# A four-layer graph network on one core: records placed by one-hot matmuls, neighbour products ahead of self products, early gathers among the scatters

## The chip, the core and the metric

The kernel runs on one core of one Trainium2 chip. The metric is the device time of one execution in microseconds (us), smaller is better. PE is the matrix engine, PEld its weight loads, DVE is VectorE, ACT is ScalarE, POOL is GpSimd, SP is the engine that issues plain DMAs. Line numbers L… are those of the kernel before.

## The reference

A graph of 3,327 nodes has 512 features per node (`x`) and a 0/1 matrix `adj` with about four ones in each row. Four layers follow one another, each as `x = x + layer(relu(layernorm(x)), adj)`:

```
layer 0:  deg = sum(adj, 1);  agg = adj @ h / max(deg, 1)
          out = relu(concat(h @ W_self + b_self, agg @ W_nb + b_nb) @ W_comb + b_comb)
layer 1:  8 heads of 64:   Wh = h @ W;  e = leaky_relu(Wh·a_src + (Wh·a_dst)^T), masked by adj
          out = softmax(e) @ Wh
layer 2:  the same with 4 heads of 128 and W made of four signed blocks; out = elu(...)
layer 3:  the same with one head of 512
```

A node without a neighbour attends in layers 1 to 3 to all nodes alike. Everything is float32.

## The kernel before, in words

The kernel never multiplies by `adj`. It finds the neighbours of each node, sorts the nodes by their number of neighbours (most first), and then gathers neighbours' rows from a table in device memory. The 3,328 rows (one is padding) are 26 chunks of 128. After sorting, `slots_of` says how many neighbour slots a chunk needs at most: 14 for chunk 0, 8 for chunk 1, 7 for 2 and 3, 6 for 4 to 6, 5 for 7 to 10, 4 for 11 to 15, 3 for 16 to 20, 2 for 21 to 23, 1 for 24 and 25; together 117. If the data does not fit these limits, a flag sends the kernel to a general path, which does not run here.

**Stage 0** (up to 264 us) works on the nodes in their given order. `SEQUENCE` (L606) is the order of the chunks. For each chunk,

- `look` (L1189) loads the rows of `adj`, and VectorE finds the columns with a one (`max_index`, L1209: four finds a chunk, 104 in all);
- `lists` (L1226), for groups of chunks, makes the node numbers from the finds and counts the degrees on VectorE; POOL writes each node's record: 16 neighbour numbers, its own number and its degree (`records`, L1259);
- `x` is loaded, normalised (statistics L1309, the refinement of 1/sigma L831 to L836), put through relu, transposed by PE (L1337), copied to `hT` (L1342) and multiplied by the two folded weights (L1349): the neighbour product goes through `zt` to `table[0]` (L1366), the self product into the node's row in SBUF (L1373). Each product is four matmuls of K = 128, which the trace shows as eight rows.

A node's row in SBUF (`node(i)`, 1,042 words) is x, self product and record. Ten chunks lie in `early`, sixteen in `later`; `later` also holds the weights while they are being folded, so these rows wait for room (`free_at`).

When all finds are done, VectorE counts the nodes of each degree with two small matmuls (L1406, L1410), and a scan and a reduction give every node's place (`places`, L1415; the result `ranki` ends the step). Then POOL scatters the 26 chunks' rows to `own` in device memory (`scatter`, L1434, one indirect DMA of 128 rows each), SP reads the records back in sorted order (`back`, L1450), and VectorE makes 1/degree from them (L1505, L1506). The places are also written beside the rows of `table[0]` (L1467), so that a gathered row brings its node's sorted place with it.

**Layer 0** (to 448 us) goes over the sorted chunks in units of one or two (`ORDERS[0]`). For each slot of a chunk POOL gathers 128 rows from `table[0]` into one of the 33 slots of `ring` (`gather`, L1545; line L1562 issues). VectorE notes the neighbours' places for the other layers (`nbr`, L1862). PE sums a part of the slots in PSUM by multiplying with the identity (`sum_on_pe`, L1584; L1593); VectorE then scales by 1/degree and adds the self product from the own row (L1871), adds the bias (L1879), adds the rest of the slots one by one (L1887; `ON_DVE` gives up to five of them to VectorE), and makes the new x (L1895). The own row (x and self product, `xy`) is loaded by SP from `own` (L1854). `project` (L1602) makes the next layer's table: statistics (L1649), normalisation, four transposes (L1694), copies (L1705), 16 rows of matmul (L1780), copies, and a store (L1822).

**Layers 1 to 3** (`attend`, L1911) gather from `table[layer]` by `nbr` after all rows of that table are stored (POOL's `mark`, L2194, waits for them). VectorE computes the softmax over the slots (L1941 to L1978), VectorE (L2110) and ACT (L2096) multiply the slots with the weights (`ON_ACT` says how many slots ACT takes), PE (and in layer 1 VectorE) sums them. In layer 3 VectorE sums, PE multiplies, and POOL scatters the result to the output (L2072).

**The order of the work** is written out at build time by `Plan` (L614): every step has an engine, a cost, a rank, what it waits for and which buffers it takes and gives; `run` repeatedly takes the step that can start first by these costs (ties by rank) and emits it. Each engine then runs its steps in that order. There is one plan for stage 0 and one for the four layers. Scatters are put behind the first plan as a list:

```
for i in SEQUENCE:
    scatter(i)
back()
degrees()
```

Of the kernel before, what the change touches and what calls it, by code (L numbers as in the profile page):

```python
# [8 lines left out]
F32 = mybir.dt.float32  # L9
# [9 lines left out]
P = 128  # L19
# [7 lines left out]
def general_path(  # L27
# [519 lines left out]
    def l3_finish(pc, i, o):  # L547
# [19 lines left out]
RING = 33  # L567
NEVER = -1.0e30
# [11 lines left out]
        (24,), (12, 21), (11,), (6,), (18,), (17,), (15,), (4,), (3,), (20,), (5, 9), (22,), (10, 19), (1,),  # L580
        (2,), (14,), (0,), (23,), (8,), (13, 16), (7,), (25,),
    ),
    1: (
        (18, 21), (22, 24), (15,), (5,), (10, 20), (2,), (17,), (12, 23), (19,), (4,), (9, 14), (7,), (11, 16),
        (8, 13), (6,), (1,), (0,), (3,), (25,),
    ),
    2: (
        (18, 23), (19, 24), (16,), (20,), (6, 11), (10, 14), (7, 12), (5, 13), (9,), (1,), (21, 22), (4,), (0,),
        (8,), (2,), (3,), (15,), (17,), (25,),
    ),  # L590
    3: (
        (0,), (7,), (17,), (15, 20), (25,), (11,), (3,), (23,), (1, 5), (24,), (4, 14), (16,), (12, 22), (8,),
        (9,), (10,), (18,), (2,), (13,), (19,), (21,), (6,),
# [5 lines left out]
    2: {S: S // 5 for S in range(1, SLOTS + 1)},  # L599
}  # L600

SUMMED = {1: False, 2: False, 3: False}
EARLY = 10
# [6 lines left out]
ORDER_W = {1: -20.0, 0: -1.0, "bias": -4.0, "later": 20.0}  # L610
ADJ, WORK, WORK0, X0, X, SELF = 1.0, 1.13, 1.2, -14.0, 1.77, 7.0


class Plan:  # L614
# [5 lines left out]
    def __init__(self, limits):  # L620
        self.ops = []
        self.limits = limits
        self.taker = {}
# [26 lines left out]
    def run(self):  # L650
        free = {}
# [41 lines left out]
def gnn_stack_kernel(  # L693
# [30 lines left out]
    ROW = 2 * D + SLOTS + 2  # L724
# [10 lines left out]
    with ExitStack() as st:  # L735
# [8 lines left out]
        own = dram.tile([NP, ROW], F32, tag="own", name="own")  # L744
# [30 lines left out]
        nc.gpsimd.iota(node_i, pattern=[[P, NK]], base=0, channel_multiplier=1)  # L775
        eps = const.tile([P, 1], F32, tag="eps", name="eps")
# [19 lines left out]
        srec_f = big.tile([P, NK, SLOTS + 2], F32, tag="srec", name="srec")  # L796
        srec = srec_f.bitcast(I32)
# [17 lines left out]

        biasf = big.tile([P, D], F32, tag="biasf", name="biasf")
# [35 lines left out]
        with tc.tile_pool(name="p0", bufs=1) as pa, tc.tile_pool(name="p0p", bufs=2, space=PSUM) as pp:  # L852
# [4 lines left out]
            early = pa.tile([P, EARLY, ROW], F32, tag="early", name="early")  # L857
            later = pa.tile([P, NK - EARLY, ROW], F32, tag="later", name="later")

            def node(i):  # L860
                return early[:, i, :] if i < EARLY else later[:, i - EARLY, :]

            spare = later.rearrange("p k w -> p (k w)")
# [5 lines left out]
            def part(name, *shape):  # L869
# [6 lines left out]
                assert spare_at[0] <= (NK - EARLY) * ROW  # L876
# [22 lines left out]
            def free_at(i):  # L899

                lo = (i - EARLY) * ROW
                return [o for (a, b), o in users if i >= EARLY and a < lo + ROW and b > lo]
# [7 lines left out]
            limits = {"ai": AI, "h": 2, "hT": 3, "pt": 2, "pz": 2, "py": 2, "pm": 2, "zt": 2, "mv": 3, "norm": 3, "st": 2, "fo": 2}  # L910
# [315 lines left out]
            def lists(rank, i0, i1, found):  # L1226
# [32 lines left out]
                def records():  # L1259
                    none = pa.tile([P, GROUP, SLOTS], F32, tag="none", name=f"none{i0}", bufs=2)[:, :n, :]  # L1260
                    nc.gpsimd.tensor_scalar(none, nid[:, i0:i1, :], 0.0, null_f[:, 1:2], ALU.is_equal, ALU.mult)
                    nc.gpsimd.tensor_tensor(none, none, nid[:, i0:i1, :], ALU.add)
                    for j in range(n):
                        rec = node(i0 + j)[:, 2 * D :].bitcast(I32)
# [4 lines left out]
                        )  # L1269

                room = [o for i in range(i0, i1) for o in free_at(i)]
                return listed, put("pool", 0.6 + 0.75 * n, rank, records, (), [listed] + room)

            recorded = {}
            listed = []
# [984 lines left out]
```

## Time and profile before

| what | us |
|---|---|
| median of 11 runs (lowest, highest) | 1072.61 (1071.53, 1078.27) |
| the profiled execution, its span | 1079.16, 1077.1 |
| PE, DVE, ACT, POOL busy | 877.9, 724.8, 518.1, 621.0 |
| last find ends; places ready | 208.4; 220.5 |
| first, last scatter | 221.6, 258.1 |
| records back, first gather | 268.6, 269.4 |
| marks: tables of layers 1, 2, 3 whole | 448.2, 653.3, 869.3 |
| last transfer to the output issued | 1065.1 |

Matmuls are pipelined and their ends are modelled: an engine's busy share is an average over stages with different limits, and a busy PE is not PE at its peak. DMA share is the mean over 16 engines.

### The profile page before, as it was taken

Reading aid. Unit: us, or ns where it says so; the run is one execution under the profiler, and the core shown is the slowest. Engines: PE = TensorE matmul, PEld = TensorE weight load, DVE = VectorE, ACT = ScalarE, POOL = GpSimd, SP = SyncE. Lnnn points to the kernel's source line nnn. Section 1 sums busy time; section 2 is a strip of 40 time slices with the busy share of each in tenths; the row PEclk is TensorE's granted clock in tenths of the full one; section 3 lists DMA queues with packets and bytes.
Section 4 is the critical chain, followed back from the end, with each engine's and each line's share of the span. In section 5 each row is a group of like instructions: output and inputs, shape, how many; then the busy total and the mean of one; then the engine's idle time right before and its main releaser. Section 6 shows DMA issues by size and latency. Waiting matters only on the chain. (4 is left out here: it accounts for less than half of the span.)

```text
span 1077.1 us, 11605 instructions
## 1 busy us (share of the span) xinstructions
PE 877.9 (82%) x2853; PEld 499.1 (46%) x2853; DVE 724.8 (67%) x1848; ACT 518.1 (48%) x1700; POOL 621.0 (58%) x719
## 2 busy tenths in 40 slices
PE   7599999995799998658999983897989815949885
PEld 4244444442376665536666652443544412414332
DVE  6399988830697769278999882787885708435541
ACT  3398877631353533436677641654664602213221
POOL 1051444673777773177787704788787057677771
PEclk9799999998899999869999996897988856979888
DMA  9999888399999986278777604767766146677671
GB/s 348 318 357 384 310 291 316 104 296 327 298 339 301 355 274 218 75 198 234 227 214 214 184 30 131 202 192 203 221 178 185 43 123 195 188 205 207 192 200 54
DMA packets 89911, 240.51 MB, mean 223 GB/s; under 512 B 24933, under 2 KB 26477, under 8 KB 89834
## 3 DMA queue, kind: packets, MB, share of 16 engines
q0 software_dynamic: 41600, 137.72, 43.3%
q1 hardware_dynamic: 48234, 101.96, 26.8%
q8 instruction: 25, 0.41, 0.2%
q14 instruction: 52, 0.43, 0.1%
HBM read 190.35 MB, written 49.27 MB: 222 GB/s over the span
## 5 line engine op out<-in xcount | busy, mean ns | idle before, releaser
L1562 POOL DMA_INDIRECT ring<-table,nbr x351 | 379.0, 1080 | 115.7 <-issue 60.4
L1593 PE MATMUL acc<-ring,ident 128*128 128x512 f32 (+1 forms) x494 | 257.3, 656 | 75.8 <-DVE ring L2110 48.5
L1780 PE MATMUL pw<-w,hT 128*128 128x264 f32 (+1 forms) x832 | 194.0, 390 | 2.1 <-ACT hT L1705 2.1
L1780 PEld LDWEIGHTS pw<-w,hT 128*128 128x128 f32 x832 | 159.8, 193 | 41.8 <-ACT hT L1705 8.5
L1593 PEld LDWEIGHTS acc<-ring,ident 128*128 128x128 f32 (+1 forms) x494 | 95.3, 208 | 180.0 <-issue 81.3
L1562 POOL DMA_INDIRECT ring<-table,srec x117 | 110.3, 943 | 45.7 <-issue 20.7
L2110 DVE TENSOR_TENSOR ring<-ring,w 128x2048 f32<-128x2048 f32 (+7 forms) x76 | 114.4, 1532 | 1.8
L1941 DVE TENSOR_TENSOR e<-ring,fs 128x24 f32<-128x24 f32 (+25 forms) x96 | 15.1, 171 | 133.6 <-DMA ring<-table,nbr 126.3
L2060 PE MATMUL pw<-w,hT 128*128 128x512 f32 x208 | 101.4, 634 | 4.2 <-ACT hT L2052 4.2
L1209 DVE FIND_INDEX8 fidx<-one_i,ai 128x8 uint32<-128x832 int32 x104 | 104.2, 1018 | 0.0
L1217 ACT ACTIVATE junk<-ai 128x1664 int8<-128x1664 int32 (+1 forms) x52 | 82.7, 1591 | 34.1 <-DMA ai<-in_adj_dram 33.8
L1349 PE MATMUL pz_n<-wf,hT_n 128*128 128x512 f32 x208 | 92.3, 595 | 2.9 <-ACT hT_n L1342 2.9
L1349 PE MATMUL py_n<-wf,hT_n 128*128 128x512 f32 x208 | 91.9, 592 | 0.0
L1705 ACT ACTIVATE hT<-pt 128x128 f32<-128x128 f32 (+1 forms) x312 | 81.9, 292 | 19.2 <-PE pt L1694 18.6
L2060 PEld LDWEIGHTS pw<-w,hT 128*128 128x128 f32 x208 | 41.8, 204 | 62.0 <-issue 48.5
L1705 ACT ACTIVATION_READ_ACCUMULATOR hT<-pt 128x1 f32 x312 | 69.4, 223 | 0.0
L822 ACT ACTIVATE ln<-mv,eps 128x1 f32<-128x1 f32 (+1 forms) x60 | 18.0, 300 | 98.5 <-DVE mv L1650 90.3
L1349 PEld LDWEIGHTS pz_n<-wf,hT_n 128*128 128x128 f32 x208 | 39.0, 190 | 52.5 <-issue 45.7
L2046 PE MATMUL pt<-ident,y 128*128 128x128 f32 x96 | 15.4, 293 | 57.6 <-DVE y L2030 52.1
L1968 ACT ACTIVATE ex<-el 128x48 f32<-128x48 f32 (+19 forms) x56 | 12.8, 232 | 101.1 <-DVE el L1951 101.1
L2194 POOL MEMSET mark<- 1x1 f32 x3 | 0.3, 88 | 106.0 <-DMA table<-t 106.0
L2030 DVE SCALAR_TENSOR_TENSOR acc<-ring,w,acc 128x512 f32<-128x512 f32 (+2 forms) x67 | 50.5, 753 | 13.6 <-ACT acc L2028 12.0
(185 smaller groups left out, 1321.0 us busy)
## 6 DMA issues: line engine op xcount, KB each, us to landing
ai<-in_adj_dram SPq DMA_DIRECT2D x25, 832.0 KB, 7.5
ai<-in_adj_dram SPq DMA_DIRECT2D x25, 831.5 KB, 7.6
table<-t SPq DMA_DIRECT2D x52, 258.0 KB, 3.6
xy<-own SPq DMA_DIRECT2D x26, 512.0 KB, 6.0
table<-t SPq DMA_DIRECT2D x26, 260.0 KB, 4.9
table<-zt_n SPq DMA_DIRECT2D x26, 256.0 KB, 5.8
ring<-table,nbr POOLq DMA_INDIRECT x351, 3.7
later<-in_x_dram SPq DMA_DIRECT2D x15, 256.0 KB, 6.8
```

The costliest lines, as they stand in the source:

```text
L822: nc.scalar.activation(ln, var, AF.Ln, bias=eps, scale=scale)
L1209: nc.vector.max_index(fidx[:, i, qq * 8 : (qq + 1) * 8], one_i, ai[:, q * QW : min(cols, (q + 1) * QW)])
L1217: nc.scalar.activation(junk[:, :cols], tiles["ai", key][:, :cols], AF.Square, accum_out=sq[:, i, hf : hf + 1])
L1349: nc.tensor.matmul(pz, tiles["hT", key][:, c, :], wf[s][:, c, :], start=(c == 0), stop=(c == DC - 1))
L1562: nc.gpsimd.indirect_dma_start(out=ring[:m, r0 + s, : width[layer]], out_offset=None, in_=table[layer], in_offset=bass.IndirectOffsetOnAxi ...
L1593: nc.tensor.matmul(acc, ident[:m, :], g[:m, s, :D], start=(k == 0), stop=(k == len(slots) - 1))
L1705: nc.scalar.activation(hT[:, c, :n], pt[:, c, :n], AF.Copy, accum_out=hsum[layer][:, i, c : c + 1])
L1780: nc.tensor.matmul(pw[:, b, :w], tiles["hT", key][:, c, :], wsb[layer][:, c, b, :w], start=(c == 0), stop=(c == DC - 1),)
L2030: nc.vector.scalar_tensor_tensor(to[:m, :], row, weight, acc[:m, :], ALU.mult, ALU.add)
L2046: nc.tensor.transpose(pt[:, c, :], tiles["y", key][:, c * P : (c + 1) * P], ident)
L2060: nc.tensor.matmul(pw[:, 0, :], tiles["hT", key][:, c, :], w3[:, c, :], start=False, stop=(c == DC - 1))
L2110: nc.vector.tensor_tensor(v, v, box["w"][:m, j, lo:hi, :].unsqueeze(3).to_broadcast([m, hi - lo, H, O]), ALU.mult,)
```

## The change

1. **Sort on chip.** The records are no longer part of a node's row. POOL writes them to `record` in SBUF as two parts: seven words (five neighbours, node number, degree) and nine more neighbours, which only the first seven sorted chunks can have. When the places are known, VectorE splits each into chunk and lane, masks the records by chunk into 245 columns, and makes a one-hot matrix of the lanes; 26 matmuls add the records up in their sorted places in PSUM; four copies bring them to `srec` and 1/degree to `rdeg`. The read `back` and `degrees` go.
2. **Rows of 1,024 words.** `own` holds x and self product alone. The ring is allocated from the start and takes the place of `later`: chunks from the eleventh of `SEQUENCE` on and the weights lie in it.
3. **Neighbour products first.** The transposed h is kept in the node's own row (where the self product later replaces it), and self products get ranks above 1000 in place of 7 behind their chunk: by the plan's rule they fill gaps and come last. 8 of the 26 stand behind the sort's matmuls.
4. **Scatters and first gathers** are emitted by their planned time. The first scattered are the chunks that lie in the ring. The gathers of the first five units of layer 0 (22 slots) stand among and behind the last scatters. POOL's order there is: 19 scatters, then a gather or two between each of the other seven, then eleven gathers. An own-row load waits for all scatters.
5. **Layer 0's first 13 units** (18 chunks, 79 slots) are summed by VectorE in the ring, one add per slot after the first; PE's sums stay for the other 8 chunks (20 of their 38 slots).
6. **Tuned numbers:** all four orders (19, 19, 16 and 20 units where there were 22, 19, 19 and 22), the ranks of loads, and `ON_ACT` of layer 2 (a third of the slots instead of a fifth). A ring slot is given back by its own reader, not by its chunk's last one. The second plan starts with engines busy for some time (`BUSY`).

```diff
+FIRST = 5
-    2: {S: S // 5 for S in range(1, SLOTS + 1)},
+    2: {S: S // 3 for S in range(1, SLOTS + 1)},
+BUSY = {"pe": 21.0, "act": 21.0, "dve": 2.0, "pool": 28.0}
+OWN_THERE = 27.0
+LEAD = 13
+AHEAD = 22
-ORDER_W = {1: -20.0, 0: -1.0, "bias": -4.0, "later": 20.0}
-ADJ, WORK, WORK0, X0, X, SELF = 1.0, 1.13, 1.2, -14.0, 1.77, 7.0
+ORDER_W = {1: -48.11, 0: -16.2, "bias": -32.92, "later": 12.95}
+ADJ, WORK, WORK0, X0, X = 1.0, 0.82, -1.09, -33.98, 4.0
...
-                    late_rank = (rank[0] + SELF, 3)
-                    y = put("pe", 3.5, late_rank, multiply, (0, "py"), [z] + finished[0], take=("py",), give=("hT",))
+                    k = SEQUENCE.index(i)
+                    late_rank = (1000.0 + k + (NK if k < EARLY else 0), 3)
+                    y = put("pe", 3.5, late_rank, multiply, (0, "py"), [z] + finished[0], take=("py",))
...
+            for k in list(range(EARLY, NK)) + list(range(EARLY)):
+                i = SEQUENCE[k]
+                rank = (1000.0 + k + (NK if k < EARLY else 0), 4)
+                o = plan.add("pool", 1.27, rank, None, [placed, own_done[i]])
+                unbound.append((o, scatter, (i,)))
+                landed[k] = plan.add("dma", 1.5, rank, None, [o], lag=1.5)
+            COLS = HEAD * NK + MORE * CAPS[FIRST]
+            PER = HW // (COLS + P)
...
+                    for lo, w, r0, nk in ((0, HEAD, 0, NK), (HEAD * NK, MORE, HEAD, CAPS[FIRST])):
+                        nc.vector.tensor_tensor(
+                            t[:, :, lo : lo + nk * w].rearrange("p i (k c) -> p i k c", k=nk),
+                            rec[:, :, r0 : r0 + w].unsqueeze(2).to_broadcast([P, n, nk, w]),
+                            at[:, :, :nk].unsqueeze(3).to_broadcast([P, n, nk, w]),
+                            ALU.mult,
+                        )
+                    nc.vector.tensor_tensor(
+                        to,
+                        box["lane"][:, k0 : k0 + n].unsqueeze(2).to_broadcast([P, n, P]),
+                        lane_i.unsqueeze(1).to_broadcast([P, n, P]),
+                        ALU.is_equal,
+                    )
...
+                        nc.tensor.matmul(
+                            box["moved"],
+                            box["to", k0][:, j, :],
+                            box["moved", k0][:, j, :],
+                            start=(k0 + j == 0),
+                            stop=(k0 + j == NK - 1),
+                        )
...
+            def arrive():
+                nc.vector.tensor_copy(srec[:, :, :FIRST], head[:, :, :FIRST])
+                nc.vector.tensor_copy(srec[:, : CAPS[FIRST], FIRST : FIRST + MORE], more)
+                nc.vector.tensor_copy(srec[:, :, SLOTS], head[:, :, FIRST])
+                nc.vector.reciprocal(rdeg, head[:, :, FIRST + 1])
...
-                load((-0.5, 0), 2e5, store_rank, (), [o])
+                rows_in.append(load((-0.5, 0), 2e5, store_rank, (), [o]))
...
+                            lo, hi = at * WIDE, (at + 1) * WIDE
+                            room = [landed[k] for k in range(EARLY, NK) if (k - EARLY) * 2 * D < hi and (k - EARLY + 1) * 2 * D > lo]
+                            o = plan.add("pool", 1.27, (2000.0, at), None, [arrived] + rows_in + room)
+                            unbound.append((o, ahead, ()))
...
-                for i in SEQUENCE:
-                    scatter(i)
-                back()
-                degrees()
+                for _, fn, args in sorted(unbound, key=lambda piece: piece[0]["at"]):
+                    fn(*args)
...
+                        ins = nc.sync.dma_start(new("xy", key, [P, 2 * D]), own[i * P : (i + 1) * P, :])
+                        for other in scattered:
+                            tc.add_manual_dep(
...
+                    lead = number < LEAD
+                    if lead:
+                        done = noted
+                        for s in range(1, S):
+                            def emit(i=i, g=g, s=s):
+                                m = held(i, s)
+                                nc.vector.tensor_tensor(g[:m, 0, :D], g[:m, s, :D], g[:m, 0, :D], ALU.add)
+                            done = plan.add("dve", 0.7, rank, emit, [done])
+                            last[s].append(done)
+                    else:
+                        summed = sum_on_pe(key, g, list(range(left)), [[o] for o in landed], rank)
```

## The prediction

> **What bounds the kernel now.** I read the table of stretches first, cut at the three marks that POOL sets when a layer's table is whole (448.2, 653.3 and 869.3 us) and at the ends of the scatters; then the waits of each engine inside layer 0; then groups by form, for durations; the chain that ended last covers 1% of the span and says nothing here.
>
> ```profile
> 222.00:265.00 43.00, 34.50 (x94) 16.12 (x92) 3.60 (x22) 11.02 (x21) 24.63 (x26) 0.95 0.96 348
> 265.00:277.00 12.00, 2.72 (x3) 1.17 (x4) 1.26 (x4) 0.00 (x0) 5.82 (x7) 0.50 0.92 252
> ...
> 300.00:350.00 50.00, 49.06 (x196) 33.94 (x195) 39.85 (x96) 23.48 (x109) 37.81 (x41) 1.00 0.96 320
> ...
> 425.00:449.00 24.00, 23.59 (x105) 17.96 (x103) 13.36 (x36) 12.94 (x66) 0.09 (x1) 1.00 0.21 78
> ```
>
> The columns are PE, PEld, DVE, ACT, POOL (busy, instructions), granted clock, DMA share, GB/s. From 222 to 265 VectorE has 3.6 of 43 us to do: the scatters and the self products run. From 265 to 277 PE stands too. In layer 0 PE is full; at its end POOL has nothing left and PE still works for 24 us.
>
> ```profile
> 264.37 0.37 SPq L1451 DMA_DIRECT2D srec<-own  x1
> 268.77 0.32 DVE L1506 RECIPROCAL rdeg<-degs 128x26 f32<-128x26 f32 x1
> 269.36 0.99 POOL L1562 DMA_INDIRECT ring<-table,srec  x1 [10.36 <-DVE rdeg L1506]
> 276.39 0.76 DVE L1871 SCALAR_TENSOR_TENSOR acc<-acc,rdeg,xy 128x512 f32<-128x512 f32 x1 [1.98 <-PE acc L1593]
> 414.06 0.95 POOL L1562 DMA_INDIRECT ring<-table,srec  x1 [0.30 <-issue]
> 448.21 0.09 POOL L2194 MEMSET mark<- 1x1 f32 x1 [33.20 <-DMA table<-t]
> ```
>
> So the records come back at 268.6, the first gather is at 269.4, the first update at 276.4, the last gather at 414.1, the table is whole at 448.2.
>
> ```profile
> L1780 PE MATMUL pw<-w,hT 128*128 128x264 f32 x416 | 96.0, 387 | 0.7 <-ACT hT L1705 0.7
> L1593 PE MATMUL acc<-ring,ident 128*128 128x512 f32 x134 | 64.9, 612 | 20.1 <-DMA ring<-table,srec 18.1 <-DVE xres L1895 1.8
> L1887 DVE SCALAR_TENSOR_TENSOR acc<-ring,rdeg,acc 128x512 f32<-128x512 f32 x39 | 29.4, 755 | 1.2
> DVE acc L1871 <- PE acc L1593: 19.7, 6, 5.3
> ```
>
> PE by its pace: a sum of one slot is two rows and comes every 0.87 us when PE is full, a projection is 16 rows in 3.72, four transposes 0.60: 67 x 0.87 + 26 x 3.72 + 26 x 0.60 = 171 of the 172 us from 276 to 448. VectorE ends its last refinement at 438.5; of the 162 us before, 28 were waits (20 for PE's sums, 8 small), so its work is 134. The mark followed 9.7 later. PE is the bound, VectorE close behind, POOL (117 gathers at 1.25 us, 146) next.
>
> The Trainium skill, Perfetto Trace Analysis, Identifying the Most-Contended Engine, would judge PE by the share of weight loads and not by busy matmuls: that is 34 of 50 us, a third free, and by it taking sums off PE is worth less than below.
>
> **Part 1, up to the places.** The finds stay on VectorE; their last ends at 208.4, the places at 220.5. In the new order all 26 chunks have their statistics ahead of the last finds, where four came after: 4 x 0.87 and two refinements of 0.76, +5.0. Four tiny operations between finds and places took 1.13 to 1.27 us beside POOL's weighing (L1131); four of that size take 0.14 to 0.25 where POOL rests, and POOL's weighing now stands ahead of the last records: -4.2. Places at 221.3; ends 212 and 228, because VectorE waited 21.3 us for adjacency in this stage and SP's order is mostly but not wholly the same.
>
> ```profile
> L1394 DVE TENSOR_TENSOR ai_sort<-degr,down_f 128x416 bf16<-128x416 f32 x1 | 0.6, 593 | 0.0
> L2110 DVE TENSOR_TENSOR ring<-ring,w 128x2048 f32<-128x2048 f32 x11 | 25.2, 2297 | 0.3
> ```
>
> **Part 2, the sort on chip.** Removed: the read of the records (264.4 to 268.6) behind all scatters. Added on VectorE: a one-hot of 676 elements and two small ones, 1.3; masks of 26 x (182 + 63 + 128) = 9,698 elements. At 1.42 ns an element (416 in 593 ns) they are 13.8, at 1.12 (2,048 in 2,297) 10.9; I take 13.1, nearer to the shorter form. Last product and its landing in PSUM 1.9, four small copies out of it about 1.0 (rows of 0.19 to 0.32). Records arrive at 238.6 (ends 225 and 250), 30 us before today. VectorE was idle there, so this costs nothing on it. On PE 26 products of 245 columns: 0.465 each by the 264-column pace, 12.1; ends 0 (PE would wait for masks anyway) and 22.6 (512 columns, 0.87). The write of places to the table (L1467), now behind the masks on VectorE and the last store on SP, is issued at 236 instead of 220.6 and lands 6.1 later by its row, 242; the first gather stands behind 19 scatters (242 to 243), so it hides; if not, each us late is a us for every scatter behind it on POOL.
>
> **Part 3, neighbour products first.** No PE work is saved. Eight self products of 3.5 us are left behind the sort's products: PE ends at 237.5 + 0.3 + 28 = 266 (256.5 today). Their copies and scatters follow one by one, with 11 gathers between; the last scatter starts at 267. Today the last started at 258.05 and all had landed by 264.4, 6.3 later: 273. The own-row loads, which need all of them, take 3.2 to 6 us: first update at 277 (ends 270 and 284), against 276.4. So the head start is not in the first update but in what is ready by then: 22 slots gathered or under way, 12 adds done.
>
> **Part 4, layer 0.** Thirteen units (18 chunks, 79 slots) are summed on VectorE in the ring: PE loses 47 of 67 sums, 41 us. VectorE: 134 - 50 x 0.775 (slots added in today's way) + 61 x 0.72 (adds) + 18 x 0.775 (other chunks) - 3 x 0.76 (fewer units) = 151, less 9 done before the first update: 142. With 7 us of waits (28 today, 20 of them for sums that PE no longer makes; ends 3 and 16), and the same 9.7 to the mark: 277 + 142 + 7 + 9.7 = 436, **12.5 less than 448.2** (ends -23 and +4). The others are earlier: PE 97 + 16 + 17 = 130; POOL 106 gathers left at 267, 132, so 399; DMA, 47 MB (gathers 26, own rows 14, table 7) at the 320 GB/s of the stretch, 146, so 413, which is near.
>
> An add has both inputs in SBUF. In layer 1, where the products with weights do, a gather takes 1,100 ns, in layer 0 943: 18 us of the products' 55 went to POOL. By that the 61 adds (43 us) cost POOL 14, 413: still early. The Trainium skill, SBUF — State Buffer, Who interferes with whom, says that such an operation and a GpSimd one that reads SBUF lock each other out for the whole instruction. By it all 43 us could fall on POOL, which would end at 442 and take the gain; no run here shows that.
>
> **Part 5, layers 1 to 3** get other orders. Layer 1 has VectorE at work nearly without a gap from 475 to 644; its first full stretch waits for 17 slots instead of 18, so nothing changes: 0 (ends -4 and +4). Layer 2: 18 slots go from VectorE (0.57 each, -10) to ACT (four of 0.32, +23, of 110 busy in 205); VectorE is busy 78% in the middle, so I take a third of it, -3 (ends -10, all; +5, ACT's copies late). Layer 3 is POOL's: 870.1 to 1050.4 for 139 transfers of 1.26, 5 of waiting; only the end moves, where the last unit has 3 slots, not 6, of 0.75: -2 (ends -6 and +3).
>
> **Sum:** -12.5 + 0 - 3 - 2 = -17.5. The profiled execution took 1079.2 (span 1077.1, 2.1 around it), so 1061.7 on it; it lies 6.5 above the median of eleven, 1072.6, and the same difference gives 1055.
>
> **Rivals.** (a) The forecast: VectorE becomes layer 0's bound; 1046 to 1066 is where its parts lead, 1055 the middle; 0.50. (b) More is free: first update at 270, waits of 3, layers 2 and 3 give up 10 and 5: -22 - 15, 1036. For it: VectorE's idle 43 us before 265 are all used; against: the own rows. 0.18, 1030 to 1046. (c) The change doesn't bring what it says: the gathers stand behind scatters that stand behind self products, DMA (0.96 share) holds layer 0 at 442 or later, and the new orders of layers 1 to 3 lose what is left, 1072; 0.18, 1066 to 1076. For it: DMA's 413 lies 13 before VectorE's end and its landing times grow under load (5.5 us against 3.7). (d) Slower: the last scatter. If moves take 22.6 and the masks stall them, PE ends near 279, the rows are in at 290, and 290 + 159 = 449 with the others at +8: 1081. It decides once the first update comes after 289, or 294 with the 5 of the other layers; 0.14.
>
> Three parts in a thousand, 3 us, is about what a measurement can tell from no change. Faster than 1069.4: (a), (b) and a third of (c), 0.74; within: 0.12; slower than 1075.8: 0.14. The range 1036 to 1076 leaves out a fifth: the lower part of (b) and most of (d).
>
> **What would show it.** Right: records out of PSUM near 239; PE's last self product near 266; first update 274 to 280; in layer 0 VectorE busy over 90% with no wait for sums, and 40 us less of ring sums on PE; mark near 436. Wrong: a first update after 285; POOL's gathers over 1.2 us in layer 0; VectorE waiting for gathers or own rows for more than 16 us; layers 1 to 3 longer than 205, 216 and 208.

## The result, and the profile after

The changed kernel is slower: 1089.93 us (median of 8 runs, 1088.64 to 1091.56) against 1073.10 us (31 runs) for the kernel before, ratio 1.015, 95% interval 1.0132 to 1.0168. The forecast was 1055, range 1036 to 1076, and slower had a chance of 0.14. In this document a ratio leaves out runs that took over 1.5% more than the fastest run of their kernel, while a median counts all. The profiled execution took 1089.05 us, span 1087.3.

The mark, which I used as the border of the layers, does not wait for the whole table: it waits for all units of a layer but the last, and layer 0's last unit now has two chunks. The border that holds in both kernels is the first gather from the next table:

| us | before | after | difference |
|---|---|---|---|
| last find ends; places | 208.4; 220.5 | 219.5; 227.6 | +11; +7 |
| records and 1/degree ready | 269.1 | 243.8 | -25 |
| last self product ends on PE | 256.7 | 270.9 | +14 |
| last scatter starts | 258.1 | 277.5 | +19 |
| first update | 276.4 | 296.3 | +20 |
| last gather, last update of layer 0 | 414.1, 436.2 | 419.6, 439.7 | +5.5, +3.5 |
| first gather of layer 1 | 452.65 | 456.34 | **+3.7** |
| layer 1, to the first gather of layer 2 | 205.0 | 217.2 | **+12.2** |
| layer 2 | 212.5 | 208.9 | **-3.6** |
| layer 3, to the end of the span | 207.0 | 204.9 | **-2.1** |

The last four sum to the 10.2 us between the two spans. The medians lie 16.8 apart; the profiled execution of the kernel before lay 6 above its median, that of the changed kernel 1 below, and these 7 us are in no row here.

The same stretches as in the prediction, from the changed kernel (PE, PEld, DVE, ACT, POOL busy; clock, DMA share, GB/s):

```profile
222.00:265.00 43.00, 43.00 (x131) 23.48 (x130) 20.02 (x50) 5.86 (x10) 31.54 (x35) 1.00 0.79 281
265.00:277.00 12.00, 5.87 (x14) 2.28 (x12) 2.89 (x6) 1.17 (x2) 9.26 (x10) 0.89 0.95 348
300.00:350.00 50.00, 42.98 (x188) 34.99 (x188) 46.98 (x110) 27.21 (x123) 38.86 (x37) 0.88 0.96 335
425.00:449.00 24.00, 22.78 (x101) 16.93 (x100) 16.62 (x42) 12.79 (x62) 0.09 (x1) 1.00 0.21 68
```

PE is no longer full in 300 to 350 and VectorE is, at 47 of 50: that is what I forecast. But look at POOL's count. It issued 37 gathers in 50 us where it had issued 41. Each is followed by 0.30 us that the busy column leaves out, so 38.86 + 37 x 0.30 = 50.0: POOL is full. So it was before: 37.81 + 41 x 0.30 = 50.1. An engine that is busy for 76% of the time by its column has no gap left here.

The marks of time from the timeline of the changed kernel:

```profile
227.46 0.18 DVE L1461 CAST ranki<-rank 128x26 int32<-128x26 f32 x1
243.53 0.31 DVE L1563 RECIPROCAL rdeg<-pm_moved 128x26 f32<-128x26 f32 x1
277.46 1.19 POOL L1473 DMA_INDIRECT own<-ring,ranki  x1 [0.30 <-issue]
281.55 0.32 SPq L1995 DMA_DIRECT2D xy<-own  x1
296.26 0.74 DVE L2037 SCALAR_TENSOR_TENSOR ring<-ring,rdeg,xy 128x512 f32<-128x512 f32 x1
419.57 0.94 POOL L1682 DMA_INDIRECT ring<-table,srec  x1 [0.30 <-DVE acc L2053]
456.34 0.95 POOL L1682 DMA_INDIRECT ring<-table,nbr  x1 [8.38 <-DMA table<-t]
```

The records are in at 243.8 and nothing before 296 makes use of it except gathers and their adds. From the first scatter (227.9) to the last gather (419.6) POOL issues 26 scatters and 117 gathers with 0.30 us between any two and no longer gap anywhere. VectorE waits meanwhile; its largest wait between 244 and the first update is for gathers (us in total, times, longest):

```profile
DVE nbr L2010 <- DMA ring<-table,srec: 43.1, 7, 19.5
```

### The profile page after: what moved, and what is told of

Its sections match the earlier page's. It is cut to its first block, busy times and chain, and to the rows that moved or that the text cites. A ratio compares the mean times of both kernels' runs of the same rounds, so it can differ in the third digit from the quotient of the medians.

```text
span 1087.3 us, 11473 instructions
## 1 busy us (share of the span) xinstructions
PE 860.5 (79%) x2811; PEld 497.8 (46%) x2811; DVE 736.0 (68%) x1848; ACT 535.5 (49%) x1755; POOL 629.2 (58%) x684
## 5 line engine op out<-in xcount | busy, mean ns | idle before, releaser
L1732 PE MATMUL acc<-ring,ident 128*128 128x512 f32 (+3 forms) x400 | 214.8, 676 | 57.6 <-DVE ring L2279 47.9
L1732 PEld LDWEIGHTS acc<-ring,ident 128*128 128x128 f32 (+3 forms) x400 | 78.9, 213 | 146.7 <-issue 67.5
L1682 POOL DMA_INDIRECT ring<-table,srec x95 | 99.0, 1042 | 28.9 <-issue 17.4
L2110 DVE TENSOR_TENSOR e<-ring,fs 128x16 f32<-128x16 f32 (+22 forms) x96 | 15.4, 170 | 144.1 <-DMA ring<-table,nbr 133.4
L2279 DVE TENSOR_TENSOR ring<-ring,w 128x2048 f32<-128x2048 f32 (+7 forms) x73 | 104.5, 1457 | 1.7
L1844 ACT ACTIVATE hT<-pt 128x128 f32<-128x128 f32 (+1 forms) x312 | 81.9, 296 | 15.2 <-PE pt L1833 14.7
L2265 ACT ACTIVATE ring<-ring,w 128x64 f32<-128x64 f32 (+1 forms) x288 | 80.1, 368 | 5.0 <-DVE w L2147 4.0
L1833 PE MATMUL pt<-ident,h 128*128 128x128 f32 x208 | 31.5, 286 | 37.0 <-ACT h L1815 36.9
L2199 DVE SCALAR_TENSOR_TENSOR acc<-ring,w,acc 128x512 f32<-128x512 f32 (+3 forms) x67 | 50.5, 754 | 13.8 <-ACT acc L2197 12.1
L1381 PE MATMUL pz_n<-wf,ring 128*128 128x512 f32 x128 | 56.8, 595 | 3.2 <-ACT ring L1374 3.2
L1942 ACT COPY t<-pw 128x512 f32<-128x512 f32 (+1 forms) x54 | 30.4, 562 | 56.2 <-PE pw L1919 52.8
```

What stands on the lines that cost most here:

```text
L1381: nc.tensor.matmul(pz, turned_h[:, c, :], wf[s][:, c, :], start=(c == 0), stop=(c == DC - 1))
L1682: nc.gpsimd.indirect_dma_start(out=ring[:m, r0 + s, : width[layer]], out_offset=None, in_=table[layer], in_offset=bass.IndirectOffsetOnAxi ...
L1732: nc.tensor.matmul(acc, ident[:m, :], g[:m, s, :D], start=(k == 0), stop=(k == len(slots) - 1))
L1833: nc.tensor.transpose(pt[:, c, :], h[:, c * P : (c + 1) * P], ident)
L1844: nc.scalar.activation(hT[:, c, :n], pt[:, c, :n], AF.Copy, accum_out=hsum[layer][:, i, c : c + 1])
L2199: nc.vector.scalar_tensor_tensor(to[:m, :], row, weight, acc[:m, :], ALU.mult, ALU.add)
```

## The experiments

Theory at the start: layer 1's loss is its new order of chunks, and layer 0's gain on VectorE exists but is eaten by its late start. Rivals: layer 1 is longer for what layer 0 leaves behind or for the lower clock; the sums on VectorE bring nothing.

### Eight runs on two other chips

The first eight ran on chips where the kernel before took 1233.2 and 1238.7 us, 15% more than the 1073 above.

**e1_order1**: the changed kernel with `ORDERS[1]` of before.

```diff
-        (2, 9), (0,), (3,), (14, 15), (23,), (25,),
+        (8, 13), (6,), (1,), (0,), (3,), (25,),
```

(the last line of the order; the others go back as well)

> The changed kernel with layer 1's order of chunks put back. Layer 1 took 205.1 us in the kernel before and 221.7 in the changed one, with the same instructions. Theory A (the new order is the cause): layer 1 falls to 203 to 209 us, the whole to 1074 (1070 to 1079). Rival B (the layer is longer for what layer 0 leaves behind, or for a lower granted clock, 0.89 against 0.93): it stays at 217 to 223 us, the whole at 1087 to 1091.

1232.29, ratio 0.9989 (0.9954 to 1.0024). Layer 1 took 239.8 from first gather to first gather. Nothing here fits either theory, since layers 1 to 3 are 29 to 37 us longer than for the same kernel on a chip of 1076 us (d1 below).

**e2_before_order1**: the kernel before with the new `ORDERS[1]`, the same diff the other way round.

> The kernel before with layer 1's new order alone. Theory A (the order is the cause): layer 1 grows from 205 to about 221 us and the whole to 1089 (1083 to 1093). Rival B (layer 0's state or the clock): the whole stays at 1073 (1070 to 1077).

1238.39, ratio 1.0033 (0.9989 to 1.0077); layer 1 took 240.0. On this chip the order makes no difference that can be measured.

**e3_ranks**: the changed kernel with the ranks of before.

```diff
-ORDER_W = {1: -48.11, 0: -16.2, "bias": -32.92, "later": 12.95}
-ADJ, WORK, WORK0, X0, X = 1.0, 0.82, -1.09, -33.98, 4.0
+ORDER_W = {1: -20.0, 0: -1.0, "bias": -4.0, "later": 20.0}
+ADJ, WORK, WORK0, X0, X = 1.0, 1.13, 1.2, -14.0, 1.77
```

> The changed kernel with the ranks of loads and transposes of the kernel before. Theory A (the last find, at 219.4 instead of 208.4, is late through these ranks, and layer 0 starts late by it): the last find ends near 209, the places are ready near 217, the mark of layer 1's table comes 7 to 11 us earlier than 447.9, the whole is 1079 to 1083. Rival B (the finds are late because POOL and VectorE have more to do ahead of them, whatever the ranks): last find 217 to 222, the whole 1087 to 1092. Rival C (earlier finds do not help since PE's self products and POOL's 48 issues set layer 0's start): last find near 209, mark within 3 us of 447.9.

1221.17, ratio 0.9857 (0.9809 to 0.9906). The last find ended at 207.0 and the places were ready at 219.1 (c2 below: 204.0 and 215.5): the ranks, not the rest of the change, put the finds 11 us later. What that costs was left to a comparable run.

**e4_lead0**: the changed kernel with layer 0's sums as before.

```diff
-LEAD = 13
+LEAD = 0
```

> The changed kernel with layer 0's sums all made as before (PE, with up to five slots of a chunk added by VectorE). Theory A (summing on VectorE gives what was forecast, and only the late start hides it): PE has 67 sums instead of 20 again, 41 us more; the mark comes at 457 to 467 instead of 447.9, the whole at 1099 to 1109. Rival B (the sums are no gain, since PE stands idle from 271 to 303 in the changed kernel and could make the sums of the early gathers there): mark within 4 us of 447.9, the whole 1086 to 1094.

1228.58, ratio 0.9956 (0.9915 to 0.9997), first gather of layer 1 at 516.1. It needs the changed kernel on such a chip beside it.

On the second of these chips the changed kernel itself ran (c0_after), e1 and e3 again (c1_order1, c2_ranks), and an experiment on VectorE's order (c3_own14):

```diff
-OWN_THERE = 27.0
+OWN_THERE = 14.0
```

> The changed kernel itself beside the kernel before, as the measure for the three that follow on the same chip. On the first chip their ratio was 1.015, with layer 1 at 221.7 us against 205.1. If this chip behaves as the first, the ratio is 1.012 to 1.018; if engines stop for 15 to 30 us without a releaser in the trace, as in the first four experiments, it may be anywhere from 0.99 to 1.01 and only differences of stages are read.

> The changed kernel with layer 1's order put back, beside the changed kernel on the same chip. Theory A (the order made layer 1 longer): 13 to 18 us less than the changed kernel, layer 1 at 203 to 209 us. Rival B (what layer 0 leaves, or the clock): within 4 us of the changed kernel.

> The changed kernel with the ranks of loads and transposes of the kernel before, beside the changed kernel on the same chip. Theory A: last find near 207, places near 218 instead of 227.6, and layer 0's mark earlier by 7 to 11 us, so is the whole. Rival C: finds and places as early, but the mark within 3 us, since PE's self products and POOL's 48 issues set layer 0's start.

> The changed kernel with the plan's time for the own rows set to 14 instead of 27, so that VectorE's first update stands ahead of the adds of the fourth to sixth unit instead of behind them. Theory A (VectorE's written order, not the arrival of the own rows, holds the first update at 296.3): it comes at 287 to 290, and the mark 3 to 8 us earlier. Rival B (the own rows are the limit: issued at 281.6, they land under load): first update 293 to 297, the mark within 3 us. Rival C: the update comes earlier but the mark does not, since VectorE still waits for the gathers of the next units.

The changed kernel itself: 1224.55 (10 runs) against 1238.67 (19 runs), 1.1% less by these medians, ratio 0.9813 (0.9750 to 0.9876). So on this chip it is **faster** than the kernel before, by between 1 and 2%. c1_order1 0.9906 (0.9859 to 0.9952), c2_ranks 0.9862 (0.9779 to 0.9945), c3_own14 0.9871 (0.9788 to 0.9954): none can be told from the changed kernel in the way expected. In c3 the first update came at 293.3 instead of 302.9, and the first gather of layer 1 at 507.1 instead of 506.0: an earlier update was worth nothing (rival C). In the traces of these two chips ACT and VectorE wait for long without a releaser that the trace names (`remote`), as here in c0_after; in those of the kernel before, the changed one and d1 there is no such wait:

```profile
336.62 0.59 ACT L1942 COPY t<-pw 128x512 f32<-128x512 f32 x1 [23.03 <-remote]
```

Up to the places stage 0 is about as long there as elsewhere (c0: last find 220.3, places 229.7); PE's last self product already ends 10 us later (281.4 against 270.9). What makes those two chips slow is not shown; I do not compare their times with the others below.

### Eight runs on chips of 1076 us

Here the kernel before took 1076.34 (25 runs) and 1075.97 us (13 runs).

**d1_order1**, as e1.

> The changed kernel with layer 1's order of chunks put back, once more, for a chip on which the kernel before takes about 1073 us. Theory A (the new order made layer 1 longer): layer 1 at 203 to 209 us instead of 221.7, the whole at 1071 to 1077, ratio to the kernel before 0.998 to 1.004. Rival B (what layer 0 leaves, or the clock): layer 1 at 217 to 223, ratio 1.011 to 1.018. Where the kernel before takes over 1200 us, as on two chips so far, layer 1 is 2 to 8 us shorter than in the changed kernel and the ratio stays 0.98 to 0.995.

1083.59, ratio 1.0053 (1.0027 to 1.0079) where the changed kernel has 1.015; layer 1 took 206.9 instead of 217.2. Theory A for the layer; the whole lies above the 1071 to 1077 that it gave. Where the time went is in the tail after layer 1's last gather, which comes 168 us after the first in both (167.9 and 167.8): 49.4 us remain in the changed kernel, 39.1 in d1. PE's projections in that tail, first of the changed kernel, then of d1:

```profile
L1919 PE MATMUL pw<-w,hT 128*128 128x260 f32 x96 | 21.9, 385 | 0.8 <-ACT hT L1844 0.8
```

```profile
L1975 PE MATMUL pw<-w,hT 128*128 128x260 f32 x64 | 17.1, 430 | 0.7 <-ACT hT L1900 0.7
```

At 16 rows a chunk, six chunks are still to be projected behind the last gather with the new order, four with the old: (14, 15), (23) and (25) stand last, behind the big chunks 2, 9, 0 and 3.

**d2_order1_ranks**: d1 with the diff of e3 as well.

> The one before with the ranks of loads and transposes of the kernel before as well. Two runs showed the last find at 203 to 207 and the places at 215 to 219 with them. Theory A (the late places cost layer 0 directly): the mark of layer 1's table 7 to 10 us earlier than in the one before, the whole as much shorter, 1062 to 1069. Rival C (PE's self products and POOL's 48 issues set the start of layer 0): mark and whole within 3 us of the one before.

1080.10, ratio 1.0037 (1.0012 to 1.0062). Places at 215.6, 12.7 us earlier than in d1; first update 296.8 against 297.6, first gather of layer 1 454.5 against 457.4. Nearly rival C: 12.7 us earlier gave 3. POOL's two longest gaps in d2 say why:

```profile
250.33 0.95 POOL L1529 DMA_INDIRECT own<-ring,ranki  x1 [4.45 <-ACT ring L1463]
260.12 0.99 POOL L1672 DMA_INDIRECT ring<-table,srec  x1 [8.84 <-DMA table<-zt_n]
```

It stood first for a self product, then for the last neighbour product's store. PE's last self product ended at 270.3 (270.9 in the changed kernel): PE's work up to there is the same, whenever the places are known.

**d3_order1_ranks_own14**: d2 with the diff of c3 as well.

> The one before with the plan's time for the own rows at 14 instead of 27, which puts VectorE's first update ahead of some adds. Theory A (the written order holds the first update): the update comes 5 to 9 us earlier than in the one before and the mark 3 to 6. Rival C (one run on a slow chip showed an update 9.6 us earlier and the mark unmoved): update earlier, mark and whole within 2 us.

1078.95, ratio 1.0012 (0.9986 to 1.0038), not to be told from the kernel before, nor from d2. First update 289.7, 7 us earlier, first gather of layer 1 at 455.9, 1.4 later. Rival C again. But this edit only puts the first update ahead of adds that stood before it: from the first to the last update VectorE is busy 137.6 us instead of 133.0 and waits 4.5 instead of 0.8. It does not show what an earlier start of all of VectorE's work would bring.

**d4_order1_lead0**: d1 with the diff of e4 as well.

> The changed kernel with layer 1's order put back and layer 0's sums made as before (67 on PE, five slots at most on VectorE). Theory A (summing on VectorE brings what was forecast): against the first of this call the mark of layer 1's table is 10 to 20 us later. Rival B (PE, idle from 271 to 302, takes the early sums there, and the sums on VectorE bring nothing): mark within 4 us.

1101.73, ratio 1.0229 (1.0181 to 1.0278); mark 467.2 against 449.7. Theory A, it seemed. Look at the durations of the gathers, though. Gathers of the kernel before, then of the changed one, then of d4 (groups by line over layer 0; count, busy, mean ns):

```profile
L1562 POOL DMA_INDIRECT ring<-table,srec x117 | 110.3, 943 | 45.7 <-issue 20.7 <-DVE rdeg L1506 10.4 <-DMA ring<-table,srec 5.2
```

```profile
L1682 POOL DMA_INDIRECT ring<-table,srec x95 | 99.0, 1042 | 28.9 <-issue 17.4 <-DMA ring<-table,srec 5.5 <-DVE ring L2037 1.8
L1616 POOL DMA_INDIRECT ring<-table,srec x22 | 21.3, 969 | 6.7 <-issue 3.0 <-DMA ring<-table,srec 1.8 <-DMA own<-ring,ranki 1.2
```

```profile
L1738 POOL DMA_INDIRECT ring<-table,srec x95 | 89.3, 940 | 51.0 <-PE acc L1788 25.4 <-issue 13.1 <-DVE acc L2109 3.7
L1672 POOL DMA_INDIRECT ring<-table,srec x22 | 21.0, 954 | 6.7 <-issue 4.3 <-DMA ring<-table,srec 1.2 <-PE py_n L1437 0.6
```

117 gathers cost POOL 110.3 us in the kernel before, 120.3 in the changed one and 110.3 again in d4, where VectorE makes no adds in the ring and again scales and updates from PSUM. In d4 POOL instead waited 25 us for PE's sums, which give the ring slots back there.

That made a new theory, N: **layer 0 is as long as POOL's row of issues**, and the change shortens this row by the gap for the records but lengthens its pieces. Still open was what holds the start at 296, so two of the next four, all from d2, moved POOL's order, one each way.

**f2_scat_first**: all scatters ahead of the first gather. **f3_lead10**: `LEAD = 10`. **f4_gath_first**: the 22 early gathers ahead of the last four scatters. **f5_last_unit**: (20, 25) cut in two.

```diff
# f2: for each gather of layer 0, an order without a wait
+    for other in scattered:
+        tc.add_manual_dep(
+            ins.ins,
+            other.ins.name,
+            mybir.DependencyInfo(mybir.DependencyClass.NoSync, mybir.DependencyReason.SCHED_ONLY),
+            reason="behind the scatters",
+        )
-    for _, fn, args in sorted(unbound, key=lambda piece: piece[0]["at"]):
+    for _, fn, args in sorted(unbound, key=lambda piece: (piece[1] is not scatter, piece[0]["at"])):
# f3
-LEAD = 13
+LEAD = 10
# f4
-    o = plan.add("pool", 1.27, (2000.0, at), None, [arrived] + rows_in + room)
+    o = plan.add("pool", 1.27, (500.0, at), None, [arrived] + rows_in + room)
# f5
-        (12,), (5, 6), (1,), (4,), (14,), (20, 25),
+        (12,), (5, 6), (1,), (4,), (14,), (20,), (25,),
```

> The changed kernel with layer 1's order and the ranks put back (1.0037 of the kernel before; first update 296.8, first gather of layer 1 at 454.5) and with all 26 scatters ahead of the first gather on POOL. Theory A (the gathers between the last scatters hold the own rows, and these the start of layer 0): last scatter near 272 instead of 275, own rows asked for at 276 instead of 279.4, first update 290 to 294, layer 1's first gather 3 to 6 us earlier. Rival B (VectorE can't start for want of gathered slots, which POOL issues at 1.25 us each): 22 gathers from 273 end at 300, first update 300 to 304, layer 1's first gather 3 to 8 us later.

1087.85, ratio 1.0111 (1.0080 to 1.0142). Rival B, beyond its numbers: the own rows were asked for 3 us earlier (276.5), the first update came at 306.9, and layer 1's first gather at 464.4, 10 later than in d2. The gathers among the scatters are a gain.

> The same base with the 22 early gathers ahead of the last four scatters on POOL. Theory A (own rows and with them the last scatter hold the start): the last scatter moves to about 292, own rows to 296, first update 303 to 306, layer 1's first gather 5 to 9 us later. Rival B (VectorE lacks gathered slots): adds end earlier, layer 1's first gather within 2 us or earlier.

1084.34, ratio 1.0086 (1.0064 to 1.0107). Theory A: VectorE waits 11.3 us for the own rows, layer 1's first gather at 461.1, 6.6 later.

```profile
303.54 0.75 DVE L2093 SCALAR_TENSOR_TENSOR ring<-ring,rdeg,xy 128x512 f32<-128x512 f32 x1 [11.27 <-DMA xy<-own]
```

So both directions lose: what is moved forward on POOL is taken from what stands behind it.

> The same base with LEAD 10 instead of 13: chunks 3, 2 and 10 are summed as before, so VectorE loses 16 adds and gets 8, PE gets 11 sums. Theory A (in the changed kernel VectorE is layer 0's only bound from the first update on, and PE has 20 us to spare): layer 1's first gather 4 to 7 us earlier than 454.5, the whole about 1074 where the base is 1080. Rival B (PE, which starts at 302, is as close): within 2 us.

1081.51, ratio 1.0060 (1.0038 to 1.0082); layer 1's first gather at 460.0, 5.5 later than in d2. Both missed. POOL's gathers were cheaper (mean 1.014 us against 1.036) and the last came at 419.7 against 420.9, but 23.7 us remained behind it instead of 16.9. VectorE had stood 5.5 us for gathers by then, 5.3 of them up to 386.5, and worked through these 23.7 without such a wait (22.1 busy). Why that wait was there was not followed up.

> The same base with layer 0's last unit (20, 25) cut in two, as the last unit was one chunk before. From the mark to the first gather of layer 1 it took 4.4 us before the change and 8.1 to 8.5 after, since the mark waits for all units but the last. Theory A (the second chunk of the last unit is one more projection and store behind the last update): 4 us from mark to first gather, and the first gather 1 to 4 us earlier than 454.5. Rival B (only the mark moves, later by as much): the first gather within 1 us.

1081.41, ratio 1.0052 (1.0035 to 1.0069); mark at 450.6, first gather at 455.0 against 454.5. Rival B: only the mark moves. It is no border to compare kernels by.

### The change's summing without the rest

**g_before_lead13**: the kernel before, with records read back and gathers behind all scatters, and of the change only the sums of 13 units on VectorE, ring slots given back one by one, `ORDERS` 0, 2 and 3, and `ON_ACT`. **g_before_lead9**: the same with nine units. In the kernel before:

```diff
+LEAD = 13
...
-                ring_readers[r0 : r0 + S] = [last] * S
+                ring_readers[r0 : r0 + S] = last
...
+                    lead = number < LEAD
...
+                                nc.vector.tensor_tensor(g[:m, 0, :D], g[:m, s, :D], g[:m, 0, :D], ALU.add)
```

The second has `LEAD = 9`.

> The kernel before, with its records read back and its gathers behind all scatters, and of the change only this: layer 0's first 13 units summed on VectorE, ring slots given back by their own readers, the orders of layers 0, 2 and 3 and ACT's third of the slots in layer 2. Theory A (the summing gains 16 us from the first update on and the change lost them by its later start): first update at 276 to 279, the last one 150 us later at 426 to 431 instead of 436, layer 1's first gather at 444 to 449 instead of 452.7, layers 2 and 3 some 4 and 2 shorter; the whole 1060 to 1068, ratio 0.987 to 0.995. Rival B (without slots gathered ahead VectorE waits for POOL's gathers, 1.25 us each, more than 16 us): last update at 436 or later, the whole 1068 to 1076.

1079.47 against 1074.01 (17 runs), ratio 1.0048 (1.0027 to 1.0069). Theory A fell; rival B holds, though the whole is longer than it said. First update, last gather and last update of layer 0:

```profile
271.69 0.75 DVE L1962 SCALAR_TENSOR_TENSOR ring<-ring,rdeg,xy 128x512 f32<-128x512 f32 x1 [0.36 <-DMA ring<-table,srec]
421.47 0.95 POOL L1620 DMA_INDIRECT ring<-table,srec  x1 [0.30 <-issue]
438.61 0.69 DVE L1986 SCALAR_TENSOR_TENSOR xres<-acc,xy 128x512 f32<-128x512 f32 x1
```

The first update came 25 us earlier than in the changed kernel, the last one at the same time. So an early start alone gains nothing. VectorE waited 17.0 us between the two, most of it for gathers (g first, then the changed kernel between its first and last update; us in total, times, longest):

```profile
DVE nbr L1935 <- DMA ring<-table,srec: 11.8, 7, 6.0
```

```profile
DVE acc L2037 <- PE acc L1732: 1.7, 2, 1.4
DVE nra L853 <- ACT r L846: 0.9, 2, 0.5
DVE nbr L2010 <- DMA ring<-table,srec: 0.2, 1, 0.2
```

The mean gather took 1.030 us in g.

> The same with nine units instead of 13 on VectorE, so that chunks 0, 3, 2 and 10 are summed as before: 16 adds fewer on VectorE, 20 sums more on PE, which has them free as it starts at 276. Theory A (work of VectorE bounds layer 0): 5 to 11 us less than with 13. Rival B (VectorE waits for PE's sums and for gathers instead, as with ten units in the changed kernel, where it cost 5.5): the same or up to 6 more.

1080.77, ratio 1.0076 (1.0050 to 1.0102). Rival B: last gather 417.1, last update 436.7, with 25.6 us of VectorE's waits between the first and the last update, 15.2 of them for gathers.

### POOL's row in all of them

A gap is what lies between two issues beyond the 0.30 us that lies between any two. Scatter and gather are means. The waits are VectorE's between its first and its last update. All in us.

| kernel | first scatter | scatter | gather | gaps | first update | waits | last gather | last update | layer 1's first gather |
|---|---|---|---|---|---|---|---|---|---|
| before | 221.6 | 0.965 | 0.943 | 14.8 | 276.4 | 24.8 | 414.1 | 436.2 | 452.7 |
| after | 227.9 | 1.115 | 1.028 | 0.0 | 296.3 | 2.8 | 419.6 | 439.7 | 456.3 |
| d1 | 228.6 | 1.108 | 1.034 | 0.0 | 297.6 | 2.6 | 420.7 | 440.8 | 457.4 |
| d2 | 215.9 | 1.106 | 1.036 | 12.7 | 296.8 | 0.8 | 420.9 | 437.9 | 454.5 |
| d3 | 217.9 | 1.106 | 1.047 | 12.6 | 289.7 | 4.5 | 424.1 | 439.3 | 455.9 |
| d4 (no adds) | 229.2 | 1.108 | 0.943 | 22.0 | 296.7 | 31.7 | 432.7 | 459.9 | 476.5 |
| f2 | 217.7 | 1.101 | 1.055 | 20.0 | 306.9 | 0.8 | 432.1 | 447.7 | 464.4 |
| f3 | 217.1 | 1.106 | 1.014 | 13.0 | 298.5 | 8.8 | 419.7 | 443.4 | 460.0 |
| f4 | 215.6 | 1.104 | 1.050 | 14.3 | 303.5 | 0.8 | 423.8 | 444.5 | 461.1 |
| f5 | 215.7 | 1.106 | 1.042 | 12.7 | 296.5 | 1.5 | 421.4 | 439.8 | 455.0 |
| g, 13 units | 218.4 | 0.964 | 1.030 | 15.1 | 271.7 | 17.0 | 421.5 | 439.3 | 456.0 |
| g, 9 units | 217.3 | 0.965 | 1.002 | 15.2 | 271.0 | 25.6 | 417.1 | 436.7 | 455.3 |

From before to after: first scatter +6.4, scatters 26 x 0.150 = +3.9, gathers 117 x 0.085 = +10.0, gaps -14.8, together +5.5, which is what the last gather shows. From d1 to d2: -12.7 and +12.7. The scatters became longer beside the sort's masks; two of the changed kernel, one beside the masks and one after them:

```profile
236.55 1.58 POOL L1473 DMA_INDIRECT own<-ring,ranki  x1 [0.30 <-issue]
243.09 0.95 POOL L1473 DMA_INDIRECT own<-early,ranki  x1 [0.30 <-issue]
```

No gap is left in the changed kernel's row. The sum up to the last gather comes out in any kernel by construction: it says where POOL's time went, not that POOL alone decides. Behind the last gather lie 15.2 (d3) to 27.2 us (d4) up to the last update, and VectorE's row has to be read beside POOL's. In the changed kernel, d1, d2, f2, f4 and f5 VectorE waits for 2.8 us or less after its first update and ends 141 to 144 us behind it, so there the first update decides: f2 and f4 put it 10.1 and 6.7 us later than d2 and end 9.9 and 6.6 later, though f4's last gather came only 2.9 later. In the two g the first update comes 25 us earlier, and VectorE waits for gathers instead and ends at 436.7 and 439.3. So POOL's row holds VectorE back at the start, or within the layer if it starts early, and VectorE's own work fills the rest: relieving one of them meets the other. Not tried is the direct proof, fewer gathers or cheaper ones; DMA (0.92 of the row's time) is near as well.

## Why the prediction was wrong, step by step

On the profiled executions the forecast was -17.5 us and the result +10.2. Of these 27.7 us layer 0, taken up to the first gather of layer 1, makes 16.2 (+3.7 instead of -12.5) and layer 1 makes 12.2 (+12.2 instead of 0).

- **Places at 221.3**: 227.6, inside the ends. The last find came 11 us later than before through the new ranks (e3, c2 and d2: 204 to 207 with the old ones), for which the forecast had no cost. With the old ranks layer 0 ends 3 us earlier (d2).
- **The sort**: right. Masks 13.3 us (13.1 forecast), products on PE 11.9 (12.1), records 16.2 after the places (17.3).
- **PE's last self product at 266**: 270.9. I counted eight products behind the sort from the forecast places. But in d2 the places come 12 us earlier and it still ends at 270.3: PE's work up to there decides, 245.8 us instead of 232.5 before, with as much idle time (25.1 us and 24.1).
- **Last scatter 267, first update 277**: 277.5 and 296.3. This is the step of layer 0's sum that failed, by 19.3 us; what I put behind it was right. I took the scatters to follow PE's copies; they followed POOL's queue, in which 11 gathers stood between them, and VectorE's first update stood behind the slots of all five early units, whose gathers came in that same row. From 244 to 296 VectorE waited 43.1 us for them. Rival (d) named this place and the point of 289, and gave 0.14; its mechanism, slow masks and products, is not what happened.
- **VectorE 142 + 7 of waits**: right: from the first update to the end of the last refinement it is 146.5 us where the forecast had 149. Of these, 143.4 lie up to the end of the last update (296.3 + 143.4 = 439.7), 2.8 of them waits. PE lost its sums as said.
- **"The others are earlier", POOL at 399, 413 with its cost**: the second step that failed, and the reason why a first update at 277 would not have brought the forecast either (g: 271.7, and the last one still at 439.3). I did count 1.25 us for each gather, but POOL's end is not the layer's: 22.1 us lay between the last gather and the last update before, and 20.1 after. By my own 413 plus 22 the last update was due at 435, and with the 12 us from there to the mark before (436.2 to 448.2) the table was due at 447, not at 436: POOL was the bound of my own sum, and next to nothing was to be gained. I compared its 146 us with the 172 of PE and left out that it starts before and ends with a tail behind it; with the 0.30 us after each issue POOL was full from its first gather to its last in both kernels. The 14.8 us of gaps, 10.1 of them for the records, were all that the sort on chip could give back on POOL. Longer gathers and scatters took 13.9 of it away again, and the later places 6.4 more.
- **What an add costs POOL**: 14 us estimated, 10.0 measured (117 gathers of 1.028 instead of 0.943). But the adds are not alone: with the sum in the ring, scaling, bias and new x of the 18 chunks read two SBUF operands too, where they had one in PSUM before. Together these are 115 operations of 80.3 us, 41.9 of them adds, so the price is an eighth of their time, not the third that I had from layer 1. By the trace, the 79 gathers of the changed kernel that overlap one of them take 1.067 us on average; the 38 others take 0.947, and none of these is over 1.01. With 74 such operations of 52.1 us (g, 9 units) the 117 gathers cost 6.9 us more than before. The Trainium skill, SBUF — State Buffer, Who interferes with whom, has such an operation and a GpSimd one that reads SBUF exclude each other, which could make it all 80; the measurement decides for an eighth. The rule named the right pair of engines, and I used its price only to say that POOL would be late at 442 if it held.
- **PE as the bound before**: g takes 47 sums off PE and layer 0 ends 3 us later than before. PE was full, but so was POOL's row. The rule of the Trainium skill that judges PE by its weight loads (Perfetto Trace Analysis, Identifying the Most-Contended Engine), by which I had less to gain from PE, was nearer to the outcome than I, but partly by luck: what took the gain was POOL, of which the row I weighed said nothing.
- **Layer 1: 0, ends -4 and +4**: +12.2, the other term that failed. I looked at the first full stretch of the new order and put its end at nothing; 10.3 of the 12.2 come from the order (d1), all in the tail, where six chunks instead of four are still to be projected. Its gathers also take 6 us longer from first to last (161.8 before; 167.9 after, 167.8 in d1, 167.9 in g), with or without the sort and the order; that part stays open.
- **Layers 2 and 3: -3 and -2**: -3.6 and -2.1, right.

On the chips of 1076 us no version beats the kernel before; d3 comes level with it.

## What to carry to other kernels

For an engine that issues indirect transfers, count instructions times the pitch from start to start (here 0.95 + 0.30 us), not its busy time; an engine at 76% may have no gap left. A stage ends at its last issue plus the tail behind it, so compare engines by end plus tail, and compare stages by a border that means the same in both kernels. When such a queue is full, moving one group of its transfers ahead only delays another, and VectorE's work with both inputs in SBUF makes its issues longer (here by an eighth of that work).

## What the runs showed of the hardware that I had not expected

Scatters on POOL took up to 1.95 us instead of 0.95 while VectorE made the sort's one-hots and masks. Gathers took 1.067 us on average where they overlapped a VectorE operation with two SBUF operands, and 0.947 where they did not. Two chips took 15% longer for the same kernel before (1233 and 1239 us against 1073 to 1076), in the traces nearly all of it behind the places. On the second of them the changed kernel was 1 to 2% faster instead of 1.5% slower; on the first it did not run. So the sign of such a change can hang on the chip, and why it does is open.
